# A conditional-expert MLP with prompt pooling: output turned to positions by 32x32 block transposes on VectorE instead of TensorE transposes

## The chip, the cores and the metric

The kernel runs on one core of a Trainium2 chip. The metric is device time in microseconds (us); lower is better. Three runs of the kernel before took 1728.20, 1728.61 and 1728.88 us, with a median of 1728.61.

## What is computed

Two blocks with residual connections, in float32, over 16 batches of 512 positions with 512 features. The first is a two-layer MLP. Of its 512 output features, 384 come from shared weights and 128 from one of 16 experts, which each batch names. The second is a pooling: every position gets a softmax-weighted sum over the positions before it, after it, or all but itself, depending on the batch's prompt type.

```python
h = gelu(einsum('bnd,hd->bnh', x, fc1_w) + fc1_b)          # 512 -> 2048
shared = einsum('bnh,sh->bns', h, fc2_w) + fc2_b           # 2048 -> 384
expert = einsum('bnh,bph->bnp', h, experts_w[idx]) + experts_b[idx]
x = x + concatenate([shared, expert], -1)

scores = einsum('bsa,a->bs', tanh(einsum('bsd,da->bsa', x, W1) + b1), v)
p = softmax(where(mask, scores[:, None, :], -1e30), -1)    # mask by prompt type
x = x + einsum('bjl,bld->bjd', p, x) / mask.sum(-1)[..., None]
```

## The kernel before

All activations lie transposed: features on the 128 partitions, the 512 positions along the free dimension. A batch's intermediate result `x1T` is a tile of 128 partitions x 4 feature blocks (`dc`) x 512 positions. The result has to be stored with positions as rows of 512 features, so it must be turned at the end.

Both MLP layers use a seven-product scheme on 2x2 blocks (seven block products instead of eight, with sums of the operands and of the results on VectorE). The first layer, `fc1_group`, runs in four groups per batch, each of seven products of four matmuls (128x128 weights, 256 positions). The second, `fc2`, has seven products of 16 matmuls each. Between its products it calls `at(name)`, at which other work is put into the engines' instruction streams. Four PSUM tiles, `ba`, `bb`, `bc` and `bd`, hold the product results. They are used again and again, each time after VectorE has read them.

The schedule is written by hand: every engine runs its instructions in the order in which the program issues them, and semaphores are placed for the data that pass between engines. The pooling of batch b is a generator (`Pooling.run_all`: `weights`, then `apply`) whose steps are drawn by `slot` calls during the first layer of batch b+1 and at `at("1")` to `at("5")` of its second layer. The pooling of the last batch has nothing to run beside, and stands alone after the last matmuls.

`apply` works on one feature block at a time with the steps `weigh`, `recur` and `finish`. `finish` (L577, L579) adds the pooled values to `x1T`. At its end L594 and L595 correct one column, that of the position with the largest score; in all batches but the last these two run on GpSimd (POOL), in the last on VectorE.

The output: `flip(t)` takes 128 positions. Four TensorE transposes through an identity matrix (L600) write a PSUM tile `py`, ScalarE copies it to a tile `yo` with two buffers (L602), and GpSimd's queue stores it (L603) as 128 rows of 2 KB. `flip(0)` and `flip(1)` of batch b are called at `at("7")` in the second layer of batch b+1, that is between its products `bd` and `ba`; `flip(2)` and `flip(3)` at `at("6")`, between `ba` and `bc`. At `at("7")` the four input sums of the next batch (`x_sums`, L121 to L124) follow on VectorE. For the last batch the four flips stand at the end of the program.

Around the output: after its second layer a batch's successor gets its expert weights by `load_expert` (L178), an indirect load on GpSimd's queue. GpSimd's queue also carries the small stores and the broadcast load of the pooling's factors (`co_d`, `cb`; L538, L539, L541), which go by SP's queue in the last batch. SP's queue loads the first layer's weights (`w`, one group ahead, two sets of buffers), the next batch's input (`xT`) and the residual's input (`xr`).

In `fc2` the sums that free PSUM for what follows are `p5x` (L343, reads `bc`), `p57` (L348, reads `bd`), `u12` and `u21` (L352 and L354, read `ba`), and the two writes of `x1T` in L355 and L356, which read `bb` and `ba`.

Of the kernel before, what the change touches and what calls it, by code (L numbers as in the profile page):

```python
# [8 lines left out]

F32 = mybir.dt.float32  # L10
I32 = mybir.dt.int32
AF = mybir.ActivationFunctionType
ALU = mybir.AluOpType
# [4 lines left out]
def tile_cond_experts_then_prompt_pool(  # L18
# [16 lines left out]
    nc = tc.nc  # L35
    P = 128
    B, _, ND, S = xT.shape
    D = ND * P
    HID = fc1T.shape[2]
    NH = HID // P  # L40
    NS = fc2T.shape[2] // P
    E, PART = exp_b.shape
    A = w1.shape[2]
    NT = S // P

    SG = 32
    SL = S // SG
# [9 lines left out]
    const = ctx.enter_context(tc.tile_pool(name="const", bufs=1))  # L57
    p1 = ctx.enter_context(tc.tile_pool(name="p1", bufs=1))
    pw = ctx.enter_context(tc.tile_pool(name="pw", bufs=2 * 7))
    ps_m = ctx.enter_context(tc.tile_pool(name="ps_m", bufs=1, space=bass.MemoryType.PSUM))  # L60
    ps_l = ctx.enter_context(tc.tile_pool(name="ps_l", bufs=2, space=bass.MemoryType.PSUM))
# [83 lines left out]
    def small(name, shape, src, dt=F32):  # L145
        t = const.tile(shape, dt, name=f"{name}_sb")
        nc.scalar.dma_start(t, src)
        return t
# [3 lines left out]
    fc2b_sb = small("fc2b", [P, NS], fc2_b)  # L152
    expb_sb = small("expb", [E, PART], exp_b)
    b1_sb = small("b1", [A, 1], b1)
# [17 lines left out]
    nc.vector.tensor_scalar(rows, idx_sb, float(P), part_f, ALU.mult, ALU.add)  # L172
    onehot = const.tile([E, B], F32, name="onehot")
    nc.vector.tensor_scalar(onehot, idx_sb[:E, :], part_f[:E, :], None, ALU.is_equal)

# [14 lines left out]
        sums(s[:, 0], s[:, 1], t[:, :KH], s[:, 2], up[:, :KH], up[:, KH:], t[:, :KH], t[:, KH:])  # L190
        return {"a22": t[:, KH:], "s1": s[:, 0], "s2": s[:, 1], "s3": t[:, :KH], "s4": s[:, 2]}


    ident = const.tile([P, P], F32, name="ident")
    make_identity(nc, ident)


    is1, not1, is2, not2, big, cnt2 = (
# [28 lines left out]

    onehot = const.tile([E, B], F32, name="onehot")
    nc.vector.tensor_scalar(onehot, idx_sb[:E, :], part_f[:E, :], None, ALU.is_equal)
    be = const.tile([PART, B], F32, name="be")  # L230
# [141 lines left out]
    class Pooling:  # L372
# [177 lines left out]
        def apply(self):  # L550
            V, b, x1T, cb = nc.vector, self.b, self.x1T, self.cb

            turn, xm = self.turn, self.xm
            c1, beta = (cb[:, ds((1 - turn) * (2 * S) + k * S, S)] for k in range(2))
            c0 = cb[:, 4 * S : 5 * S]
            fac, kap, gam = (cb[:, 5 * S + k : 5 * S + k + 1] for k in range(3))
            T = p1.tile([P, ND], F32, tag="T", name=f"T_{b}")
            U = p1.tile([P, ND], F32, tag="U", name=f"U_{b}")
            f, u, v = {}, {}, {}

            def turned(t):
                return t[:, ds(turn * S, S)]

            def weigh(dc):
                u[dc] = p1.tile([P, 2 * S], F32, tag="u", name=f"u_{b}_{dc}", bufs=2)
                V.tensor_tensor(u[dc][:, :S], x1T[:, dc, :], c1, ALU.mult)  # L566
                nc.scalar.activation(u[dc][:, S:], u[dc][:, S - 1 :: -1], AF.Identity, accum_out=T[:, dc : dc + 1])  # L567
                yield 0.65

            def recur(dc):  # L570
                f[dc] = p1.tile([P, S], F32, tag="f", name=f"f_{b}_{dc}", bufs=3)
                V.tensor_tensor_scan(f[dc], c0, turned(u[dc]), 0.0, ALU.mult, ALU.add)  # L572
                offset(dc)
                yield 1.35

            def finish(dc):
                V.tensor_tensor(f[dc], turned(v[dc]), beta, ALU.mult)  # L577
                yield 0.65
                V.tensor_tensor(x1T[:, dc, :], x1T[:, dc, :], f[dc], ALU.add)  # L579
                yield 0.65  # L580

            def offset(dc):
                V.tensor_scalar(U[:, dc : dc + 1], T[:, dc : dc + 1], kap, xm[:, dc : dc + 1], ALU.mult, ALU.add)  # L583
                v[dc] = p1.tile([P, 2 * S], F32, tag="v", name=f"v_{b}_{dc}", bufs=2)
                nc.scalar.activation(v[dc][:, :S], f[dc], AF.Identity, bias=U[:, dc : dc + 1], scale=fac)  # L585
                nc.scalar.copy(v[dc][:, S:], v[dc][:, S - 1 :: -1])  # L586

            for step, dc in (
                (weigh, 0), (weigh, 1), (recur, 0), (weigh, 2), (recur, 1), (finish, 0),
                (weigh, 3), (recur, 2), (finish, 1), (recur, 3), (finish, 2), (finish, 3),  # L590
            ):
                yield from step(dc)
            E = self.eng
            E.tensor_tensor(T, T, gam.to_broadcast([P, ND]), ALU.mult)  # L594
            E.tensor_tensor(self.x_max, self.x_max, T, ALU.add)  # L595

        def flip(self, t):
            py = ps_l.tile([P, ND, P], F32, tag="y", name=f"py_{self.b}_{t}")
            for dc in range(ND):
                nc.tensor.transpose(py[:, dc, :], self.x1T[:, dc, ts(t, P)], ident)  # L600
            yo = p1.tile([P, D], F32, tag="yo", name=f"yo_{self.b}_{t}", bufs=2)
            nc.scalar.copy(yo, py.rearrange("p k d -> p (k d)"))  # L602
            nc.gpsimd.dma_start(out[self.b, ts(t, P), :], yo)  # L603

    t2 = None
    pool = None
    for b in range(B):
# [3 lines left out]
        hT = p1.tile([P, NH, S], F32, tag="hT", name=f"hT_{b}")  # L611
# [53 lines left out]
        pool = Pooling(b, x1T)  # L665
    pool.project()
    pool.score()
    while not pool.done:
        pool.slot(1e9)
    for t in range(NT):  # L670
        pool.flip(t)


# [40 lines left out]
```

## Time and profile before

| | us |
|---|---|
| median of the runs | 1728.61 |
| profiled execution, in all | 1730.4 |
| its span, first to last instruction | 1728.6 |
| TensorE transposes of the output (L600), 256 | 34.8 busy |
| ScalarE copies of the output (L602), 64 | 34.5 busy |
| issues of the output's stores (L603), 64 | 34.8 on GpSimd's queue |
| output store, from issue to landing | 2.3 to 3.8, median 2.6 |
| HBM read and written | 180.68 MB and 21.07 MB |

The page lists each engine's busy time, its share of the span, and the groups of instructions with their mean duration and what they waited for. PE is TensorE (PEld its weight loads), DVE is VectorE, ACT is ScalarE, POOL is GpSimd and SP is the engine that only issues DMAs. A name such as `SPq` is that engine's queue. The mean granted TensorE clock is 0.985 of full speed. One batch takes about 104 us.

In the part of the page that shows the span in 40 slices, the last slice and the one before it look different from the others: TensorE has next to nothing left, and what remains is the pooling of the last batch.

```
PE   7999999999999999999999999999999999999990
DVE  4627456282653827447283563827547283563815
ACT  2205134251432415234150432515234160332513
```

### The profile page before, as it was taken

The numbers are of one execution on the slowest core, as the hardware profiler recorded it, in microseconds if no ns is written. First come the engines' busy times: TensorE is split into PE (matmuls) and PEld (weight loads), VectorE is DVE, ScalarE is ACT, GpSimd is POOL, SyncE is SP. The second block draws the span as 40 slices with busy tenths as digits, with TensorE's granted clock in tenths as the row PEclk, the third lists the DMA queues.
The fourth block names the chain that finished last, engine by engine and source line by source line (L and its number), as shares of the span: only waits on it lengthen the run. The fifth ranks groups of instructions, "written<-read, shape, count | busy, mean of one in ns | idle before, by whom it ended". The sixth has DMA issues, their size and how long they took to land. (4 is left out here: it accounts for less than half of the span.)

```text
span 1728.6 us, 21107 instructions
## 1 busy us (share of the span) xinstructions
PE 1665.2 (96%) x7596; PEld 1419.3 (82%) x7596; DVE 909.3 (53%) x1690; ACT 557.9 (32%) x1137; POOL 125.0 (7%) x194
## 2 busy tenths in 40 slices
PE   7999999999999999999999999999999999999990
PEld 6888888888888888888888888888888888888870
DVE  4627456282653827447283563827547283563815
ACT  2205134251432415234150432515234160332513
POOL 1000000000000000100000000000100000000000
PEclk8999999999999999999999999999999999999995
DMA  8324343333523334343333533335343343533201
GB/s 280 128 92 141 104 150 95 114 113 106 181 92 110 116 111 145 104 135 94 120 122 104 176 99 104 121 107 152 104 117 99 127 128 104 165 103 103 63 31 43
DMA packets 141579, 203.21 MB, mean 118 GB/s; under 512 B 14355, under 2 KB 101411, under 8 KB 139427
## 3 DMA queue, kind: packets, MB, share of 16 engines
q1 hardware_dynamic: 126082, 150.78, 28.7%
q0 software_dynamic: 11824, 49.67, 7.8%
q10 hardware_dynamic: 3568, 1.41, 0.3%
q8 instruction: 61, 1.00, 0.2%
q14 instruction: 44, 0.35, 0.1%
HBM read 180.68 MB, written 21.07 MB: 117 GB/s over the span
## 5 line engine op out<-in xcount | busy, mean ns | idle before, releaser
L241 PE MATMUL ba<-xT,w_a 128*128 128x256 f32 x1024 | 242.0, 379 | 2.0 <-DMA w_a<-in_fc1T 2.0
L241 PEld LDWEIGHTS ba<-xT,w_a 128*128 128x128 f32 x1024 | 194.5, 190 | 29.1 <-issue 2.7
L267 ACT ACTIVATE hT<-c,fc1b_sb 128x256 f32<-128x256 f32 x384 | 172.1, 501 | 82.3 <-DVE c L298 47.9
L319 ACT ACTIVATE xr<-xr,fc2b_sb 128x256 f32<-128x256 f32 x96 | 43.3, 498 | 302.7 <-DMA xr<-in_xT 302.7
L241 PE MATMUL ba<-hT,fc_sb 128*128 128x256 f32 x512 | 114.8, 382 | 12.5 <-ACT hT L267 12.5
L241 PE MATMUL bc<-xs,w_a 128*128 128x256 f32 x512 | 122.9, 383 | 3.8 <-DVE u L281 3.8
L241 PE MATMUL bb<-xs,w_s 128*128 128x256 f32 x512 | 122.4, 382 | 2.8 <-DVE w_s L77 2.8
L241 PE MATMUL bd<-xs,w_s 128*128 128x256 f32 x512 | 122.5, 382 | 0.0
L241 PE MATMUL bd<-xT,w_s 128*128 128x256 f32 x512 | 122.2, 382 | 0.0
L241 PEld LDWEIGHTS ba<-hT,fc_sb 128*128 128x128 f32 x512 | 96.0, 190 | 30.9 <-ACT hT L267 18.5
L241 PE MATMUL bc<-xs,w_s 128*128 128x256 f32 x512 | 121.3, 380 | 0.0
L241 PEld LDWEIGHTS bb<-xs,w_s 128*128 128x128 f32 x512 | 98.0, 191 | 23.1 <-issue 7.2
L241 PEld LDWEIGHTS bd<-xs,w_s 128*128 128x128 f32 x512 | 96.0, 190 | 25.4 <-PE bc L241 13.0
L267 ACT ACTIVATE hT<-ba,fc1b_sb 128x256 f32<-128x256 f32 x128 | 53.5, 469 | 194.3 <-PE ba L241 194.3
L241 PE MATMUL bd<-hT,exp 128*128 128x256 f32 x512 | 115.7, 379 | 0.0
L241 PE MATMUL bd<-hT,fc_lo 128*128 128x256 f32 x512 | 115.7, 379 | 0.0
L241 PE MATMUL bb<-hT,fc_sb 128*128 128x256 f32 x512 | 113.1, 379 | 0.0
L241 PEld LDWEIGHTS bc<-xs,w_a 128*128 128x128 f32 x512 | 98.2, 192 | 18.1 <-DVE u L281 4.6
L273 ACT COPY p1s<-ba 128x512 f32<-128x512 f32 x64 | 36.7, 574 | 234.9 <-PE ba L241 232.4
L241 PEld LDWEIGHTS bd<-xT,w_s 128*128 128x128 f32 x512 | 98.3, 192 | 13.8
L241 PEld LDWEIGHTS bc<-xs,w_s 128*128 128x128 f32 x512 | 97.7, 191 | 13.4
L241 PEld LDWEIGHTS bd<-hT,exp 128*128 128x128 f32 x512 | 97.3, 190 | 13.2
(158 smaller groups left out, 2398.5 us busy)
## 6 DMA issues: line engine op xcount, KB each, us to landing
w_s<-w1s_s SPq DMA_DIRECT2D x240, 256.0 KB, 2.8
w_a<-in_fc1T SPq DMA_DIRECT2D x189, 256.0 KB, 2.9
xT<-in_xT SPq DMA_DIRECT2D x64, 256.0 KB, 4.7
xr<-in_xT SPq DMA_DIRECT2D x64, 256.0 KB, 3.3
out_y<-yo POOLq DMA_DIRECT2D x64, 256.0 KB, 2.6
cb<-co_d POOLq DMA_DIRECT2D x15, 769.5 KB, 4.9
w1s_s<-w_s POOLq DMA_DIRECT2D x16, 256.0 KB, 4.1
fc_sb<-in_fc2T SPq DMA_DIRECT2D x1, 2048.0 KB, 12.6
```

The costliest lines, as they stand in the source:

```text
L241: nc.tensor.matmul(bank[:, m, :], w(m, k), mv[:, k, :], start=(not add and m == 0 and k == 0), stop=(k == depth - 1), skip_group_check=True,)
L267: nc.scalar.activation(hT[:, hc, ts(c, HC)], src[:, m, :], AF.Gelu, bias=fc1b_sb[:, hc : hc + 1])
L273: nc.scalar.copy(p1s, ba)
L319: nc.scalar.activation(t[:, m, :], t[:, m, :], AF.Identity, bias=bias)
```

## The change

The identity matrix, the TensorE transposes, the PSUM tile `py` and ScalarE's copy are removed. `flip` now takes a feature block `dc` instead of a block of positions. One VectorE instruction transposes the 128x512 slice `x1T[:, dc, :]` within its 32x32 blocks into a tile `yo` of the same size. In `yo`, partition 32a + j holds, for each of 16 blocks c, the 32 features 128 dc + 32a + (0 to 31) of position 32c + j. Four DMAs, one for each 32 partitions, store it in pieces of 32 features, 128 bytes.

Where the calls in the loop stand is unchanged: two flips at `at("7")`, two at `at("6")`, now with the meaning of feature blocks 0, 1 and 2, 3. Their DMAs stay on GpSimd's queue, and `yo` keeps two buffers.

In the last batch `flip(dc)` is called inside `apply`, after each `finish(dc)`. The correction of the one column is made there for each feature block with one VectorE instruction on 128x1 elements. The four blocks have a buffer each (in the space of `hT`), and their DMAs alternate between SP's and ScalarE's queues.

```diff
-    ident = const.tile([P, P], F32, name="ident")
-    make_identity(nc, ident)
...
                 yield from step(dc)
-            E = self.eng
-            E.tensor_tensor(T, T, gam.to_broadcast([P, ND]), ALU.mult)
-            E.tensor_tensor(self.x_max, self.x_max, T, ALU.add)
-
-        def flip(self, t):
-            py = ps_l.tile([P, ND, P], F32, tag="y", name=f"py_{self.b}_{t}")
-            for dc in range(ND):
-                nc.tensor.transpose(py[:, dc, :], self.x1T[:, dc, ts(t, P)], ident)
-            yo = p1.tile([P, D], F32, tag="yo", name=f"yo_{self.b}_{t}", bufs=2)
-            nc.scalar.copy(yo, py.rearrange("p k d -> p (k d)"))
-            nc.gpsimd.dma_start(out[self.b, ts(t, P), :], yo)
+                if self.last and step is finish:
+                    at = self.x_max[:, dc : dc + 1]
+                    V.scalar_tensor_tensor(at, T[:, dc : dc + 1], gam, at, ALU.mult, ALU.add)
+                    self.flip(dc)
+            if not self.last:
+                E = self.eng
+                E.tensor_tensor(T, T, gam.to_broadcast([P, ND]), ALU.mult)
+                E.tensor_tensor(self.x_max, self.x_max, T, ALU.add)
+
+        def flip(self, dc):
+            if self.last:
+                if dc == 0:
+                    self.yo = p1.tile([P, NH, S], F32, tag="hT", name="yo_last")
+                yo = self.yo[:, dc, :]
+            else:
+                yo = p1.tile([P, S], F32, tag="yo", name=f"yo_{self.b}_{dc}", bufs=2)
+            nc.vector.transpose(yo, self.x1T[:, dc, :])
+            to = out[self.b].rearrange("(c j) (k a i) -> k a j c i", j=32, a=4, i=32)
+            for a in range(4):
+                queue = (nc.sync, nc.scalar)[a % 2] if self.last else nc.gpsimd
+                queue.dma_start(to[dc, a], yo[ts(a, 32), :].rearrange("j (c i) -> j c i", i=32))
...
-    for t in range(NT):
-        pool.flip(t)
```

More of the change, by code (lines that the diff above doesn't have):

```diff
@@ L6 @@
 from concourse.bass import ds, ts
-from concourse.masks import make_identity
 from concourse._compat import with_exitstack
@@ L43, in tile_cond_experts_then_prompt_pool @@
     A = w1.shape[2]
-    NT = S // P
     SG = 32
```

## The prediction

> **What bounds the kernel now.** I read the page's first part, then a timeline of the end of one batch's second layer, then the last 75 us, then what the output's own instructions cost.
>
> ```profile
> PE 1665.2 (96%) x7596; PEld 1419.3 (82%) x7596; DVE 909.3 (53%) x1690; ACT 557.9 (32%) x1137; POOL 125.0 (7%) x194
> ```
>
> TensorE is busy for 96% of the span, and so sets the pace until its last batch ends. A busy share can hide waits, so the next view is the timeline of 180 to 220 us (start, length, engine, line, operation), the stage in which the transposes of batch 0 lie inside the second layer of batch 1:
>
> ```profile
> 192.24 0.69 DVE L343 TENSOR_TENSOR p5x<-bc,xr 128x512 f32<-128x512 f32 x1 [4.67 <-PE bc L241]
> ...
> 195.44 3.62 PE L241 MATMUL bd<-hT,exp 128*128 128x256 f32 x16
> ...
> 198.89 1.04 PE L600 MATMUL py<-ident,x1T 128*128 128x128 f32 x8
> 199.09 0.69 DVE L348 TENSOR_TENSOR p<-bd,p5x 128x512 f32<-128x512 f32 x1 [3.63 <-PE bd L241]
> ...
> 199.76 3.62 PE L241 MATMUL ba<-hT,fc2s 128*128 128x256 f32 x16
> ...
> 206.67 1.04 PE L600 MATMUL py<-ident,x1T 128*128 128x128 f32 x8
> 206.93 0.69 DVE L352 TENSOR_TENSOR u<-ba,xr 128x512 f32<-128x512 f32 x1 [7.15 <-PE ba L241]
> ...
> 207.54 3.62 PE L241 MATMUL bc<-hT,fc2s 128*128 128x256 f32 x16
> ...
> 208.73 0.68 DVE L356 TENSOR_TENSOR x1T<-ba,p 128x512 f32<-128x512 f32 x1
> ```
>
> The matmuls run without a gap. Lengths overlap, so starts count: eight transposes take 199.76 - 198.89 = 0.87 us of TensorE's time, and 207.54 - 206.67 = 0.87 us again. VectorE waits 3.63 us before L348 and 7.15 us before L352.
>
> The chain of waits that ended last, and the timeline of the tail, show that after 1679 us one batch's pooling runs alone. Its end:
>
> ```profile
> 1717.31 0.69 DVE L579 TENSOR_TENSOR x1T<-x1T,f 128x512 f32<-128x512 f32 x1
> 1717.91 0.16 DVE L594 TENSOR_TENSOR T<-T,cb 128x4 f32<-128x4 f32 x1
> 1718.11 0.17 DVE L595 TENSOR_TENSOR x1T<-x1T,T 128x4 f32 x1
> ...
> 1724.57 0.54 POOL L603 DMA_DIRECT2D out_y<-yo  x1 [0.33 <-ACT yo L602]
> ```
>
> In the waits of SP's queue the final wait for `out_y` is 27.5 us; it starts when SP's last DMA issue ends (1698.96 + 0.36), so the last output lands at 1726.8.
>
> **What the Trainium skill says.** (1) "VectorE: DVE Perf Modes", section The three transpose paths: VectorE transposes only inside 32x32 blocks and writes SBUF, TensorE transposes 128x128 whole but into PSUM. Nothing here contradicts it; the groups by line hold small block transposes, which price the large ones:
>
> ```profile
> L474 DVE STREAM_TRANSPOSE wt<-wm 32x128 f32<-32x128 f32 x16 | 4.8, 300 | 0.5
> L451 DVE STREAM_TRANSPOSE mt<-ml 32x32 f32<-32x32 f32 x16 | 3.2, 199 | 0.6
> ```
>
> (2) "DMA: Bandwidth & Descriptors", section Specifications: transfers under 512 B lose line rate, because the engine then reads, modifies and writes. No row of this trace isolates 128 B stores; their price is my largest unknown. (3) Same page, section Anatomy of one DMA: many descriptors can be emitted on the GpSimd path before the added cost shows. The trace agrees over its small span: an output issue of 128 pieces takes 542 ns on POOL (L603), the one of a single 12-byte piece (L539) 542 ns. (4) Same page, section Issuing engines are not separate DMA queues: issues from SP, ACT and POOL share the same 16 engines. So the tail's spread over two queues divides issue time, not transfer time.
>
> **The change part by part.** *Removed in the loop:* 15 batches have their transposes inside the next batch's second layer, two stretches of 0.87 us each: 15 x 2 x 0.87 = 26.1 us of TensorE. What follows each stretch has its operands ready: `hT` was combined by 182.8 us (L336), and `bc` was freed by L343 at 192.9. I take 26.1 us as gained whole. The 60 PSUM copies on ACT (0.59 us each) and the identity's construction go too, at no gain: ACT is 32% busy and none of these copies is on TensorE's path.
>
> *Added on VectorE in the loop:* from 32 to 128 columns a transpose grows by (300 - 199)/96 = 1.05 ns per column, so 512 columns cost 0.300 + 384 x 0.00105 = 0.70 us. The order of the built program puts the first two between L343 and the four `xs` sums, the others between L348 and L352. 1.4 us fits in each of the 3.63 and 7.15 us idle stretches: no cost. Without that cover it is 1.4 us a time. `x1T` is final by 177.8 (L595 on POOL, 175.66 + 2.10).
>
> *Added wait:* `yo` has two buffers, so transpose 2 waits until the four DMAs of transpose 0 have landed, and transpose 3 for those of 1. Behind them on VectorE stand L352, L354, L355 and L356, and the next batch's first `ba` product waits for these to read `ba`. Two products of 6.91 us (starts 207.54, 214.45) lie after L352's release, so that product starts at 221.36 now, and at 219.6 once this batch's two stretches are gone. The four sums take 2.5 us and transpose 3 takes 0.7: the DMAs of transpose 1 must have landed by about 216.3. The first can issue at 193.6, which leaves 22.7 us for 8 DMAs. With 1.6 us of fixed latency (an output of 8 pieces of 2 KB per engine lands in 2.3 us at least, about 0.7 of it transfer), and 5.2 us of engine time for the 2.1 MB of loads that SP issues from 192.96 to 196.8 (16 engines at the 0.040 ns a byte found below), 15.9 us remain for 256 pieces per engine: 62 ns a piece.
>
> *Price of a 128 B piece.* Each block of 128 features now makes 4 x 32 x 16 = 2048 pieces, 128 per engine. Low end, from the queue table:
>
> ```profile
> q1 hardware_dynamic: 126082, 150.78, 28.7%
> q0 software_dynamic: 11824, 49.67, 7.8%
> ```
>
> Share x 1728.6 x 16 / packets is 63 ns at 1196 B for q1 and 182 ns at 4200 B for q0. A straight line through both gives 15.4 ns + 0.040 ns per byte, so 20.5 ns at 128 B. High end: the store of 96 pieces of 64 B (L538) lands in 3.1 us from POOL, the single piece (L539) in 2.7; issue accounts for 0.09 of that, leaving 0.31 us for five more pieces per engine if all 16 share it: 62 ns. I take the middle, 41 ns, because [...]part of the low end ignores that these are small stores to HBM.
>
> At 41 ns the 256 pieces take 10.5 us, well within 15.9: no stall. The 16 POOL issues per batch I take at 0.65 us (L538 with its three dimensions takes 0.63); they would decide only at 2.5 us each. `load_expert` (L178) is queued behind them on POOL. It issues at 221.8 and its tile is first used some 25 us later, with a landing of 5.7 us, so it has slack. Weight loads run one group of 12 us ahead and land in 2.8 us; sharing the engines costs nothing.
>
> *The tail.* After the last batch `flip` runs inside `apply`, once per `finish`, and a 128x1 correction replaces L594/L595. Each insertion is about 0.2 + 0.7 = 0.9 us on VectorE. VectorE is busy from 1705.7 to 1716.4, so the first two delay the last `recur` by 1.8; the third stands while ACT makes `v` for the last block (L585 and L586, 1715.01 to 1716.48), and about 0.75 of it shows. The last L579 then ends at 1720.5 instead of 1718.0, the last transpose at 1721.3. The two DMA issues per block on ACT, about 0.5 us each as L404 takes, stand behind the transposes and before work that waits on VectorE anyway. What goes is the end: TensorE 1.1, ACT, and two rounds of DMAs on two `yo` buffers, 8.8 us from 1718.0 to 1726.8.
>
> On the timeline of before, so without the 26.1 us, block 0 is out of VectorE at about 1711.2 (L579 of `finish` 0 ends at 1710.3, plus 0.9), so its pieces start at 1711.95 and the engines then have 4 x 128 pieces. At 41 ns that is 21.0 us: 1732.95, and with 0.9 us of receipt 1733.85, 7.05 later than 1726.8. The transfers, not VectorE, end the kernel: blocks arrive 2 to 4 us apart and each takes 5.2.
>
> **Sum.** -26.1 + 7.05 = -19.05 us on the profiled span of 1728.6: 1709.5. The profiled run took 1730.4 in all, and the median of the runs is 1728.61; I apply the same difference to the median and forecast 1709.5.
>
> **Rivals.** *A, cheap pieces (20.5 ns):* a block takes 2.6 us, less than the spacing, so only the last shows: issues at 1721.35 and 1721.85, 1.6 us of latency and about 2.3 of transfer, landing at 1725.8, 1 us earlier than before. Total -27.1: 1701.5. The queue table is for it; that it comes from large pieces is against.
>
> *B, dear pieces (50 to 62 ns) that still don't stall the loop:* at 62 the tail's pieces take 31.7 us and end at 1744.6, +17.8; total -8.3: 1720.3. The L538/L539 difference is for it.
>
> *C, slower:* one mechanism, the wait of transpose 3 for `yo`. Above 62 ns every ns adds 0.256 us of stall in each of 15 batches, 3.8 us in all, besides 0.5 in the tail. The gain is gone at about 64 ns (15 x 0.5 = 7.7, tail 18.8, together 26.5), and at 75 ns it costs 15 x 3.3 = 50 plus 24.5 in the tail: 1777. POOL's issues at over 2.5 us would open the same stall, at 15 x 8 = 120 us for each further us. Against it: no issue on POOL takes over 1.04 us, and 62 is the ceiling of my estimate.
>
> *D, the freed TensorE time isn't gained* because something else ends the stage: 1728.6 + 7 = 1735.7. Against it, matmuls start back to back on both sides of the transposes.
>
> **Chances.** Forecast (27 to 50 ns) 0.57, A 0.19, B 0.09, C 0.12, D 0.03. A change of 0.2%, 3.5 us, is what a measurement tells from none. Faster: forecast, A, B, less a margin at B's end, 0.83; within 0.2%: 0.03; slower: C and D less the same margin, 0.14. The range is 1700 to 1724: A's end with 1.5 us for VectorE's tail, and B's end with 4 us of stalls.
>
> **What would show it.** Right: no `py`, and matmuls of L241 back to back across the two places; transposes of 128x512 at 0.70 us; no TensorE wait at the first `ba` of a batch; a final wait for `out_y` that outlasts the last transpose by over 10 us. The queue table prices the pieces: q0's packets should rise by 15 x 8192 = 122,880, q1's and q10's together by 8192. Wrong: VectorE waiting for `out_y` before the third or fourth transpose until past 216 us on this timeline (C), POOL issues of several us, or an end within 5 us of the last transpose (A).

## The result, and the profile after

The changed kernel takes 1700.26 us (median of 6 runs, 1697.89 to 1702.04), the kernel before 1728.74 (6 runs, 1726.56 to 1731.25): 28.5 us less, a ratio of 0.9834 with a 95% interval of 0.9821 to 0.9846. The forecast was 1709.5 in a range of 1700 to 1724. The direction and the main term held; the measured time lies at the very bottom of the range (two of the six runs lie below 1700), next to rival A's 1701.5. The profiled execution has a span of 1698.5 us.

The page of the changed kernel, first its busy times, then its DMA queues (packets, MB, share of 16 engines):

```profile
PE 1636.2 (96%) x7340; PEld 1392.1 (82%) x7340; DVE 951.7 (56%) x1756; ACT 523.6 (31%) x1073; POOL 245.6 (14%) x368
```

```profile
q1 hardware_dynamic: 130306, 151.31, 29.4%
q0 software_dynamic: 14384, 48.63, 9.9%
q10 hardware_dynamic: 7792, 1.93, 0.5%
```

TensorE is busy for 29 us less and still for 96% of a shorter span: the bound has stayed where it was. GpSimd is busy for twice as long, since it now issues 240 stores at 0.65 us instead of 64 at 0.54. q1 and q10 (SP's and ScalarE's queues) have 4224 packets more each, as 4096 pieces and 8 DMAs' completions on 16 engines would give. q0, GpSimd's queue, has only 2560 more, although 122,880 pieces went over it: packets there are not pieces, as the probes below show.

The timeline of the same stage that the prediction showed, batch 0's output inside the second layer of batch 1:

```profile
191.31 1.29 DVE L606 STREAM_TRANSPOSE yo<-x1T 128x512 f32<-128x512 f32 x2
...
192.31 5.21 POOL L610 DMA_DIRECT2D out_y<-yo  x8 [16.08 <-DVE yo L606]
...
193.90 3.62 PE L236 MATMUL bd<-hT,exp 128*128 128x256 f32 x16
...
197.35 3.62 PE L236 MATMUL ba<-hT,fc2s 128*128 128x256 f32 x16
...
199.33 0.71 DVE L606 STREAM_TRANSPOSE yo<-x1T 128x512 f32<-128x512 f32 x1 [1.09 <-DMA out_y<-yo]
...
202.83 0.71 DVE L606 STREAM_TRANSPOSE yo<-x1T 128x512 f32<-128x512 f32 x1 [2.79 <-DMA out_y<-yo]
...
204.26 3.62 PE L236 MATMUL bc<-hT,fc2s 128*128 128x256 f32 x16
204.51 0.69 DVE L347 TENSOR_TENSOR u<-ba,xr 128x512 f32<-128x512 f32 x1 [0.97 <-PE ba L236]
...
206.32 0.68 DVE L351 TENSOR_TENSOR x1T<-ba,p 128x512 f32<-128x512 f32 x1
...
218.07 1.89 PE L236 MATMUL ba<-xT,w_a 128*128 128x256 f32 x8
```

(L347 and L351 are L352 and L356 of the kernel before, L236 is L241.) The two places of the transposes are closed: `ba` starts 3.45 us after the last half of `bd`, and so does `bc` after the last half of `ba` (200.80). The third and fourth transposes do wait for the stores, 1.09 and 2.79 us, but L347 still waits 0.97 us for TensorE afterwards: the wait ends before the thing behind it is due. L351 is done at 207.0, and TensorE needs it at 218.07.

How long a batch takes is read from the starts of the second layer's first product. For the kernel before in batches 0 and 15, then for the changed kernel (durations in ns, then first to last start in us):

```profile
L241 PE MATMUL ba<-hT,fc_sb x32: 379/379/483, 68.8 to 75.6; 128*128 128x256 f32 x32
L241 PE MATMUL ba<-hT,fc_sb x32: 379/379/483, 1628.9 to 1635.7; 128*128 128x256 f32 x32
```

```profile
L236 PE MATMUL ba<-hT,fc_sb x32: 379/379/483, 67.3 to 74.0; 128*128 128x256 f32 x32
L236 PE MATMUL ba<-hT,fc_sb x32: 379/379/483, 1602.9 to 1609.7; 128*128 128x256 f32 x32
```

1560.1 us against 1535.6: 24.5 us less in 14 periods that hold a batch's transposes, 1.75 us each. The fifteenth lies in the second layer of batch 15 itself, so the loop gives 26.2 us. The first start differs by 1.5 us, which is not the change's: over the profiles of this study it lies anywhere from 65.2 to 68.8, at 65.6 in a kernel that has the change in its last batch alone, and what moves is how many of the first matmuls run at half speed after TensorE's early waits (eight matmuls in 3.2 to 3.8 us instead of 1.9: three such groups in the kernel before, one in `double_transpose`, whose start is the one at 65.2). These 1.5 us account for the difference between the two profiled spans (30.1 us) being larger than that between the medians (28.5).

The tail, from the timeline, and the last landing, from the waits of SP's queue:

```profile
1692.93 0.22 DVE L590 SCALAR_TENSOR_TENSOR x1T<-T,cb,x1T 128x1 f32 x1
1693.18 0.71 DVE L606 STREAM_TRANSPOSE yo_last<-x1T 128x512 f32<-128x512 f32 x1
```

```profile
SPq L715 <- DMA out_y<-yo_last: 2.2, 1, 2.2
```

SP's last issue ends at 1694.8, so the output has landed at about 1697.0, 3.1 us after the last transpose. From the first product of `apply` (1676.37) that is 20.6 us, against 22.65 before (1704.15 to 1726.8).

### The profile page after: what moved, and what is told of

It is laid out like the page before. It is cut to its first block, busy times and chain, and to the rows that moved or that the text cites. A ratio compares the mean times of both kernels' runs of the same rounds, so it can differ in the third digit from the quotient of the medians.

```text
span 1698.5 us, 20848 instructions
## 1 busy us (share of the span) xinstructions
PE 1636.2 (96%) x7340; PEld 1392.1 (82%) x7340; DVE 951.7 (56%) x1756; ACT 523.6 (31%) x1073; POOL 245.6 (14%) x368
## 3 DMA queue, kind: packets, MB, share of 16 engines
q1 hardware_dynamic: 130306, 151.31, 29.4%
## 4 chain that ended last, share of the span: by engine, by line
PE 84%; DVE 7%; ACT 3%; issue 2%; DMA 2%; DVEq 1%; SPq 0%; ACTq 0%
PE bd L236 23%; PE bc L236 23%; PE ba L236 23%; PE bb L236 11%; PE pa L383 3%; DVE f L567 3%; ACT hT L262 1%; DMA w_a<-in_fc1T 1%; PE psc L392 1%; DVE u L561 1%; ACT v L580 1%; DVE f L572 1%; DVE c L293 1%; DVE u L276 1%; ACT u L562 1%
## 5 line engine op out<-in xcount | busy, mean ns | idle before, releaser
L236 PE MATMUL ba<-xT,w_a 128*128 128x256 f32 x1024 | 243.8, 381 | 1.9 <-DMA w_a<-in_fc1T 1.9
L236 PEld LDWEIGHTS ba<-xT,w_a 128*128 128x128 f32 x1024 | 195.6, 191 | 29.3 <-issue 2.6
L610 POOL DMA_DIRECT2D out_y<-yo x240 | 155.1, 654 | 294.3 <-DVE yo L606 288.1
L236 PE MATMUL ba<-hT,fc_sb 128*128 128x256 f32 x512 | 114.8, 382 | 12.5 <-ACT hT L262 12.5
L236 PE MATMUL bc<-xs,w_a 128*128 128x256 f32 x512 | 122.8, 383 | 3.2 <-DVE u L276 3.2
L236 PE MATMUL bb<-xs,w_s 128*128 128x256 f32 x512 | 122.8, 383 | 1.0 <-DVE w_s L75 1.0
L236 PE MATMUL bd<-xs,w_s 128*128 128x256 f32 x512 | 122.5, 382 | 0.0
L236 PE MATMUL bc<-xs,w_s 128*128 128x256 f32 x512 | 121.4, 380 | 0.0
L236 PEld LDWEIGHTS ba<-hT,fc_sb 128*128 128x128 f32 x512 | 96.0, 190 | 31.0 <-ACT hT L262 18.5
L236 PE MATMUL bd<-xT,w_s 128*128 128x256 f32 x512 | 120.9, 379 | 0.0
L236 PEld LDWEIGHTS bd<-xs,w_s 128*128 128x128 f32 x512 | 96.0, 190 | 25.4 <-PE bc L236 13.0
L236 PEld LDWEIGHTS bb<-xs,w_s 128*128 128x128 f32 x512 | 98.3, 192 | 21.7 <-issue 7.2
L236 PE MATMUL bd<-hT,fc_lo 128*128 128x256 f32 x512 | 115.7, 379 | 0.0
L236 PE MATMUL bd<-hT,exp 128*128 128x256 f32 x512 | 115.7, 379 | 0.0
L236 PE MATMUL bb<-hT,fc_sb 128*128 128x256 f32 x512 | 113.1, 379 | 0.0
L236 PEld LDWEIGHTS bc<-xs,w_a 128*128 128x128 f32 x512 | 98.2, 192 | 17.5 <-DVE u L276 4.0
L272 DVE TENSOR_TENSOR u<-bb,p1s 128x512 f32<-128x512 f32 x64 | 43.8, 684 | 119.6 <-PE bb L236 119.3
L236 PEld LDWEIGHTS bc<-xs,w_s 128*128 128x128 f32 x512 | 97.8, 191 | 13.5
```

The source lines that it names most:

```text
L236: nc.tensor.matmul(bank[:, m, :], w(m, k), mv[:, k, :], start=(not add and m == 0 and k == 0), stop=(k == depth - 1), skip_group_check=True,)
L272: nc.vector.tensor_tensor(u2, bb, p1s, ALU.add)
L610: queue.dma_start(to[dc, a], yo[ts(a, 32), :].rearrange("j (c i) -> j c i", i=32))
```

## The experiments

### Each half of the change alone

```diff
 # loop_only: the last batch as before; nothing of flip inside apply
...
+    for t in range(4):
+        pool.flip_pe(t)
 # tail_only: the loop as before
...
-                        pool.flip(t)
+                        pool.flip_pe(t)
```

`flip_pe` is the `flip` of the kernel before (L600 to L603), put back beside the new one together with the identity matrix.

> The change in the first 15 batches alone; the last batch is turned by TensorE transposes as before. Theory: freed TensorE time of 15 x 1.75 us is the gain and the 128-byte pieces in the loop are hidden, so 26 us less than before, 1702.5 us, and a tail as before (22.6 us from the first product of apply to the last landing). Rival (part of the gain came from the end of the kernel or from its start): clearly less than 26, down to 24 us less.

> The change in the last batch alone. Theory: pieces are cheap (about 13 ns each), so the tail is 2 us shorter than before: 1726.6 us, and the last landing comes 3 us after the last transpose. The prediction's price of 41 ns would make it 7 us longer: 1735.7 us. The low price of 20.5 ns: 1 us shorter.

`loop_only` took 1702.44 us against 1728.87 of before, ratio 0.9845 (0.9832 to 0.9859): 26.4 us less. `tail_only` took 1727.05, ratio 0.9987 (0.9980 to 0.9994): 1.8 us less. Together 28.2, the whole of the change. Both theories hold. For the loop the profile is sharper than the medians: in `loop_only` the starts of the second layer's first product run from 66.7 in batch 0 to 1602.3 in batch 15, the same 1535.6 us as in the changed kernel. The prediction's tail, 7 us longer, is refuted by the second run.

### More work for VectorE

```diff
-            nc.vector.transpose(yo, self.x1T[:, dc, :])
+            for _ in range(1 if self.last else 2):
+                nc.vector.transpose(yo, self.x1T[:, dc, :])
```

> The changed kernel with each block transpose in the loop made twice: 60 x 0.64 = 38 us more of VectorE's work, 2.6 us a batch. Theory (it lies in VectorE's idle stretches): 1700 us within 2. Rival (VectorE stands on the path there): 15 x 2.6 = 38 us more.

1700.48 us (1698.43 to 1701.55): no change. (Beside these and the following experiments the kernel before took 1728.7 to 1729.1, so the changed kernel's 1700.26 serves as their measure.) The groups by line, the changed kernel first, show that the work is there and doubled (busy us, mean ns, idle before):

```profile
L606 DVE STREAM_TRANSPOSE yo<-x1T 128x512 f32<-128x512 f32 x60 | 40.8, 698 | 44.5 <-DMA out_y<-yo 44.5
L607 DVE STREAM_TRANSPOSE yo<-x1T 128x512 f32<-128x512 f32 x120 | 82.8, 703 | 43.7 <-DMA out_y<-yo 41.5
```

### The wait for `yo`: below and above its limit

The threshold was worked out on the changed kernel: L351 ends about 3.1 us after the fourth transpose starts, and TensorE needs it at 218.07, so the transpose must start by 214.9. Three kernels move that start with smaller pieces, fewer buffers, or both.

```diff
 # half_2buf
+                for h in range(1 if self.last else 2):    # two DMAs of 64-byte pieces
+                    w = ds(0, 32) if self.last else ts(h, 16)
...
 # full_1buf: pieces as in the change
-                yo = p1.tile([P, S], F32, tag="yo", name=f"yo_{self.b}_{dc}", bufs=2)
+                yo = p1.tile([P, S], F32, tag="yo", name=f"yo_{self.b}_{dc}", bufs=1)
 # half_1buf: both
```

> The changed kernel with every piece in the loop cut into two of 64 bytes, stored by twice as many DMAs (32 a batch, 0.65 us of issue on GpSimd each). Theory: the fourth transpose then waits until about 205.5 us on the timeline of the changed kernel, where it has until 214.9 before TensorE must wait: no change, 1700 us within 2. Rival (pieces cost 41 ns or more each whatever their size, as the prediction had it): 512 pieces per engine for the first two blocks take 21 us, the fourth transpose comes at about 216 or later, and the kernel is at least 15 us slower.

> The changed kernel with one buffer for yo and the pieces of 128 bytes as they are. Theory: each block now waits for the one before it, about 2.6 us of issue and some 3 of landing and turning, so the fourth transpose of a batch starts at about 211 us on the timeline of the changed kernel, before the 214.9 from which TensorE must wait: no change, 1700 us within 2. Rival (any longer wait on yo is paid for, with or without the slack): the three waits of 1 to 7 us each show in part, and the kernel is 15 us slower or more.

> As half_2buf, but with one buffer for yo in place of two, so that each transpose waits for the landing of the block before it. Theory (the wait decides once the fourth transpose starts after 214.9 us): each block costs 5.2 us of issue and some 3 us of landing and turning, the fourth transpose starts at about 217, and TensorE waits some 2 us at the first product of each of 15 batches: 20 to 50 us slower than the changed kernel, about 1731 us. Rival (the wait on yo has no part in the time): 1700 us.

`half_2buf` took 1700.49 us, with the fourth transpose at 204.74, and `full_1buf` 1698.90: no change in either. `half_1buf` took 1752.92 (1749.40 to 1762.17): 53 us slower than the changed kernel and 24 slower than the kernel before (ratio over the runs 1.0157, 1.0129 to 1.0184), on the other side of the line. The timelines of `full_1buf` and then `half_1buf` at the same place, the fourth transpose and what stands behind it:

```profile
210.70 0.71 DVE L606 STREAM_TRANSPOSE yo<-x1T 128x512 f32<-128x512 f32 x1 [4.58 <-DMA out_y<-yo]
...
213.10 0.68 DVE L351 TENSOR_TENSOR x1T<-ba,p 128x512 f32<-128x512 f32 x1
...
217.94 1.89 PE L236 MATMUL ba<-xT,w_a 128*128 128x256 f32 x8
```

```profile
214.26 3.62 PE L236 MATMUL bd<-hT,exp 128*128 128x256 f32 x16
218.11 0.71 DVE L606 STREAM_TRANSPOSE yo<-x1T 128x512 f32<-128x512 f32 x1 [7.34 <-DMA out_y<-yo]
...
220.52 0.68 DVE L351 TENSOR_TENSOR x1T<-ba,p 128x512 f32<-128x512 f32 x1
...
221.29 3.65 PE L236 MATMUL ba<-xT,w_a 128*128 128x256 f32 x8 [3.42 <-issue]
```

With the fourth transpose at 210.70 nothing is lost, although VectorE's waits for `out_y` are five times as long as in the changed kernel. From the waits, the changed kernel first, then `full_1buf` (us in all, times, longest):

```profile
DVE yo L606 <- DMA out_y<-yo: 44.5, 29, 3.1
DVE yo L606 <- DMA out_y<-yo: 215.0, 45, 8.7
```

With it at 218.11 L351 ends at 221.2, and TensorE starts at 221.29 instead of 217.7. (Its wait is marked "issue", which means that the profile shows no releaser; that it is L351 follows from the two times and from `ba`, which L351 reads.) So rival C's mechanism is real and its place was right. The limit itself, 214.9, is worked out; the runs show that it lies between 210.70 and 218.11.

The cost was a little above my 20 to 50 us. The waits of `half_1buf` give the stall (us in all, times, longest), and two later batches, at the same product, show the rest:

```profile
PE ba L236 <- issue: 36.0, 14, 3.4
```

```profile
328.41 1.96 PE L236 MATMUL ba<-xT,w_a 128*128 128x256 f32 x8 [2.82 <-issue]
...
538.56 3.59 PE L236 MATMUL ba<-xT,w_a 128*128 128x256 f32 x8 [2.36 <-issue]
```

The stall is 2.6 us on average over the 14 that are listed, near what I expected. In 5 of the 14 batches the eight matmuls after it take 3.3 to 3.65 us instead of 1.96: they run at about half speed. The period from batch 1 to batch 15 is 105.8 us, 3.4 more than the changed kernel's 102.4. The profiled execution is the fastest of the four, 49 us longer than the changed kernel's: 36 us of it are these stalls and some 8 the slow matmuls, and the rest is not traced. The two slowest executions, 1756.2 and 1762.2 us, show a lower mean granted clock (0.977 and 0.975, against 0.982), as more batches with slow matmuls would give; they have no trace.

### The price of a piece by itself

The changed kernel with 64 stores more at its end, to scratch memory; nothing of the result is left out.

```diff
+    for n in range(64):
+        r, dc, a = n // 16, n // 4 % 4, n % 4
+        to = room[r].rearrange("(c j) (k a i) -> k a j c i", j=32, a=4, i=32)[dc, a]
+        src = pool.yo[ts(a, 32), dc, :].rearrange("j (c i) -> j c i", i=32)
+        (nc.sync, nc.scalar)[n % 2].dma_start(to, src)   # probe_pool_128: nc.gpsimd
 # probe_hw_2k: whole rows of 2 KB, [32, 512] to [32, 512], in place of the rearranged pieces
```

> The changed kernel with 64 further stores behind its last block, alternately on SP's and ScalarE's queues, of the last batch's four blocks to scratch memory, each in 512 pieces of 128 bytes as in the change: 2048 more pieces per engine with nothing beside them. Theory (12 to 13 ns a piece, as the shares of the queue table after the change give): the time grows by some 26 us. The prediction's 41 ns would give 84 us, its low end of 20.5 ns 42 us, its high end of 62 ns 127 us.

> The same 64 stores with the same bytes in 32 pieces of 2 KB each. Theory: 128 pieces per engine at the line of the queue table (15.4 ns + 0.040 ns a byte, 97 ns) take 12.5 us, and 32 issues of 0.42 us on each of two queues take 13.4: some 13 us more than the changed kernel. What probe_hw_128 takes beyond this is the price of the small pieces. Rival (the bytes or the issue set the time, not the pieces): both probes take the same.

> The 64 stores in pieces of 128 bytes again, all from GpSimd's queue. Theory: in the records its pieces travel together, 16 to a packet, so they cost no more than on the other queues, and the issue of 0.65 us each sets the time: 64 x 0.65 = 42 us more. Rival (each piece costs 41 ns or more on this queue): 84 us or more.

They took 1729.70, 1717.37 and 1737.11 us, so 29.4, 17.1 and 36.9 more than the changed kernel's 1700.26. From the timelines of `probe_hw_128`, then `probe_hw_2k`, the stretch in which each queue issues its 32 stores:

```profile
1693.53 29.39 SPq L682 DMA_DIRECT2D room<-yo_last  x32
1693.60 29.42 ACTq L682 DMA_DIRECT2D room<-yo_last  x32
```

```profile
1695.22 17.23 SPq L682 DMA_DIRECT2D room<-yo_last  x32
1695.29 17.35 ACTq L682 DMA_DIRECT2D room<-yo_last  x32
```

With whole rows an issue comes every 0.54 us (I had taken 0.42). The DMA engines are then busy for 86 to 92% of the time, and SP's 32 issues include 2.7 us of waits for earlier stores, so neither issue nor transfer alone sets the time, and this probe gives no clean price for a row. With small pieces an issue comes every 0.92 us. That the issue itself is longer with 512 pieces is ruled out: in the changed kernel's tail two such issues on ScalarE's queue take 0.95 us together, at 1683.62, with nothing ahead of them. The transfers hold the queue back: from 1695 to 1724 the DMA engines are busy for 98 to 100% of the time and move 140 to 144 GB/s, against 250 to 255 with whole rows from 1700 to 1713.

29.4 us over 2048 pieces per engine is 14.4 ns a piece, data included. The theory (26 us) is close, and all three of the prediction's prices are too high. On GpSimd's queue 41 of the 64 stores follow one another at 0.64 us each, so issue sets most of the time; the first started on blocks that were ready before the last, hence less than 42 us. Queue table of `probe_pool_128`:

```profile
q0 software_dynamic: 16432, 52.83, 11.5%
```

11.5% of 16 engines over its span of 1735.3 us, less 9.9% over 1698.5, is 503 us for 32,768 pieces: 15.3 ns each, near the 14.4 of the other queues and far from 41.

## Why the prediction was right in sign and too cautious in size

- **Freed TensorE time, 26.1 us:** 26.2 in the trace, 26.4 in `loop_only`. The difference of starts, not the transposes' busy time (34.8 us for all 256), was the right number.
- **Transposes on VectorE, 0.70 us and hidden:** 0.698 us; hidden, and twice the work would be too.
- **The wait for `yo`, due by about 216:** the fourth transpose started at 202.83. The limit, 216.3 on the old timeline, is 214.9 on the new one, where the batch starts earlier. It lies between 210.70, which costs nothing, and 218.11, which costs a wait of TensorE at the product that was named.
- **POOL's issues, 0.65 us:** 0.65. `load_expert` behind them issued without delay, at 218.52, right after TensorE released its tile.
- **VectorE in the tail:** the last transpose ends 17.5 us after the first product of `apply`; 17.15 was worked out.
- **The step that failed is the price of a 128-byte piece, 41 ns; measured 14.4.** The four blocks' pieces then take 1.8 us each instead of 5.2, less than the 2.3 us and more between them, so they never queue up. The output lands 3.1 us after the last transpose instead of 12.5, and the tail became 2 us shorter instead of 7 longer. That is 9 us, as much as lies between 1709.5 and 1700.26. Both ends of the bracket lay above the truth. The high end came from one difference of landing times between two small stores; what it holds besides the price of pieces, no run here separates. The low end came from a line through two averages of large packets, whose intercept of 15.4 ns alone exceeds what a whole small piece takes; the upper of its two points, q0's 4200 B, stands for packets of several pieces and not for a piece (last section). Taking the middle of two estimates that err the same way did not help.
- **q0's packets, expected to rise by 122,880:** wrong, since that queue's packets hold many pieces.

What happened is rival A (1701.5), down to the sign that the prediction named for it, an end within 5 us of the last transpose; A's own price of 20.5 ns was still too high. That the measured time lies inside the stated range is in part luck: the lower end stood at A's outcome with 1.5 us to spare, and the median clears it by 0.26 us.

What the Trainium skill says in "DMA: Bandwidth & Descriptors", section Specifications, that transfers under 512 B lose line rate, agrees with the probes as far as it goes: 14.4 ns for 128 B is 142 GB/s over 16 engines, while the same bytes in rows of 2 KB moved at 250 to 255. The price in the prediction would have been 50 GB/s (128 B in 41 ns). Whether the engine reads and modifies before it writes no run here shows.

## What to carry to other kernels

Work that the bounding engine does for layout alone was worth its start-to-start time in every pass here (0.87 us a stretch), not its busy time (1.04). Move it to an engine whose idle stretch lies at that place, and check what stands behind the moved instruction when it waits. Before giving up long rows for short pieces, price the pieces by themselves (64 stores to scratch memory behind the end of the kernel suffice) instead of extrapolating from large ones, and work out the latest time at which the stores may land. Here stores that landed before it cost nothing, and later ones cost the whole wait and, in some batches, slow matmuls behind it.

## What was not expected of the hardware

- **A short stall can slow what follows, and its length does not tell whether it will.** In `half_1buf` the eight matmuls after the stall took 3.3 to 3.65 us in five batches, after 1.97, 2.36, 2.84, 3.22 and 3.42 us without matmuls, and 1.96 or 1.97 in nine, after 1.66 to 3.26 us. The granted clock fell behind the pause and not in it: 1.00 from 217.9 to 221.2, 0.50 over the slow matmuls from 221.3 to 224.7, and 1.00 over the fast ones from 328.4 to 330.2. What decides between the two is open.
- **GpSimd's queue carries many pieces in a packet, SP's and ScalarE's one.** `probe_hw_128` has 16,896 packets more on q1 than the changed kernel for 32 stores, 528 each: 512 pieces and 16. `probe_pool_128` has 2048 more on q0 for 64 stores, 32 each, which would be one packet of 32 pieces (4 KB) and one completion for each of 16 engines (inferred from the counts; the 16 to a packet that I had expected come from counting the completions as packets of data). The 480 DMAs of `half_2buf` give 32 each too, so there a packet holds the 32 pieces of 64 B, 2 KB. The stores of before, 8 rows of 2 KB per engine, gave 80 each (`tail_only` has 320 packets on q0 less for four of them), which fits four packets of 4 KB and a completion. The page "DMA: Bandwidth & Descriptors" of the Trainium skill, section SWDGE vs HWDGE vs iDMA, gives 4096 B as the preferred upper size of a packet, in agreement. Packing made a piece little cheaper, if at all: 15.3 ns by the queue's share on GpSimd's queue, and 16.8 by the same reckoning for the two others (30.0% and 1.4% of 1727.0 us against 29.4% and 0.5% of 1698.5); the shares' rounding alone can shift each by 1 to 2 ns.
